# Mixing two expert branches as (x + a) + g (e − a), with −a added in PSUM and the ternary weight made at a later place

## The chip, the cores and the metric

The kernel runs on one core of a Trainium2 chip. The core has a matrix engine (PE), a vector engine (DVE), an activation engine (ACT), a general engine (POOL) and an engine that mainly issues transfers (SP). The metric is the device time of one launch in microseconds (us). All numbers here are us unless they say otherwise. A row such as `128x1024 f32` means 128 partitions with 1024 elements each.

## The reference, cut to what matters

Two layers on an input of 2 sequences of 2048 rows, 256 wide, all in float32. In the first layer attention and a mixture of experts work side by side on the normalised input; in the second a Mamba state space and a linear layer with a ternary weight do.

```python
xn = layernorm(x)
# first layer, feed-forward half (xn is normalised once more inside, with ln_g, ln_b)
abel   = gelu(xn2 @ abel_w + abel_b)                 # "a" in this text
moe    = sum over the two chosen experts of weight * expert(xn2)
nonabel = moe @ rot                                  # "e"; rot is a product of three matrix exponentials
g      = sigmoid(concat([abel, nonabel]) @ mix_w + mix_b)
ffn    = xn + abel * (1 - g) + nonabel * g
x      = x + attention(xn) + ffn

# second layer
xn = layernorm(x)
delta  = 0.7 * mean(abs(weight))
w_tern = where(weight > delta, 1, where(weight < -delta, -1, 0)) * alpha
x      = x + mamba(xn) + (xn @ w_tern.T + bias)
# mamba: projection to 1024, causal convolution over 4 rows, silu, projections for dt, B and C,
# a scan h = exp(dt A) h + dt B x over the rows for 512 channels and 16 states, y = sum h C + x D, gate, projection
```

## The kernel before, in words

Rows are tiled as 32 tiles of 128 rows, grouped in eight chunks of 512 rows (`QT` = 4 tiles). Four stages follow each other.

**The first stage** (0 to 183 in the profiled execution; the lines 180 to 319) loops over the eight chunks c. Each chunk is normalised twice (`n1`, `n2`; `normalised` at L144 issues four DVE tensor_scalar operations), transposed, and projected to q, k and v, which leave for DRAM or stay in SBUF. Its branch a is made by matmuls (L300, L307) and a GELU on ACT (L308) into `ab`. Then POOL multiplies `ab` by the gate's weights into `am` (L311), DVE sums `am` over its columns into `sab` (L314), SP spills `ab` to the DRAM array `ab_d` (L315), and POOL adds `n1` and the attention bias to the kept input `xa` (L316, L317). The buffers `ab` and `am` belong to a pool that ends with the stage; the next stage's constants lie in the same area.

**Attention** (183 to 1229) makes masks first (L595 to L635, on POOL) and then runs units written out by hand: the maxima of one unit (L665, L675, L678) are issued 22 units ahead of the exponentials and the values of another. SP reads q and k from DRAM for it (L554). It adds its result to `xa`.

**The experts** (1229 to 1876) take 37 tiles of gathered rows through two matrices of one expert each and write the results to `y_d`. `xa` goes out to `xa_d` there.

**Mixing and state space** (1876 to 3025; L1167 to L1893) works on eight units, one per chunk of 512 rows, the two sequences in turn. Three generators do the work of a unit: `mix(at)` gathers the experts' rows, scales and adds them, computes the gate and the mixed rows, and normalises and transposes them; `ahead(at)` projects, convolves and makes dt, B and C; `behind(at)` gates, projects and writes the output. The scan itself is a loop over 128 steps (8 units of 16 steps). In each step DVE runs a scan of 128x2048 (L1862) and the product that feeds a later one (L1772), POOL multiplies by C (L1874), PE sums over the states (L1789), and `steps(at, n, q)` advances the generators of the units that are one, two and three ahead at places in a table.

The order of the work has two regimes. Up to the line `ctx.enter_context(tc.manual_schedule())` (L1803) a planner orders each engine's instructions by program order and its own costs. Behind that line every engine, and every queue of transfers, runs in program order. What is issued there first is: all of `mixes[0]`; ten alternating pieces of `aheads[0]` and `mixes[1]` (its eight gathers and the scaling); the piece of `aheads[0]` that makes dt for the first 128 channels (L1513 to L1522); the 16 loads of C's rows by SP (`c_rows`, L1720); three more pieces of `mixes[1]` (POOL's sum L1335, the loads of `ab` and `xc` L1337 and L1339, and the transposes L1346); and a piece of `aheads[0]` that fills four blocks of a spreading matrix (DVE, L1526) and spreads dt by matmuls (L1536). Then comes the first step of the scan.

Inside `mix`, the gate's logits go through ACT (L1367, L1368) and a DVE reciprocal (L1374) to g, ACT forms 1 − g (L1375), PE multiplies the experts' rows by `rot` in two halves `pn` (L1381; one float32 matmul is two instructions in the trace), DVE adds g times each tile of `pn` to `xc` (L1388), ACT scales `ab` by 1 − g (L1395, four operations), and POOL adds it to `xc` (L1398). DVE's statistics (L1404) follow.

The ternary weight is made once, by the lines 1261 to 1275 in the setup ahead of the planner's end: a load of 256 KB on SP, an absolute value on ACT (L1264), a sum on DVE (L1266), a matmul with ones (L1268), and six DVE operations (L1270 to L1275). Its buffer `wt` shares a single place (tag `k`) with `ab` of each unit and with each unit's `n3`. Its first reader is the output projection of the first unit (L1621).

Of the kernel before, what the change touches and what calls it, by code (L numbers as in the profile page):

```python
# [11 lines left out]
F32 = mybir.dt.float32  # L12
F32R = mybir.dt.float32r
AF = mybir.ActivationFunctionType
ALU = mybir.AluOpType
AX = mybir.AxisListType
# [3 lines left out]
P = 128  # L20
B = 2
S = 2048
D = 256
# [78 lines left out]
def tile_model(ctx: ExitStack, tc: tile.TileContext, t, out):  # L102
    nc = tc.nc
# [15 lines left out]
    ident = const.tile([P, P], F32, name="ident")  # L119
    make_identity(nc, ident)  # L120
    ones = const.tile([P, P], F32, name="ones")
    nc.gpsimd.memset(ones, 1.0)
    rot = const.tile([P, 2, D], F32, name="rot")
# [27 lines left out]
    QT = CH // P  # L151
# [6 lines left out]
    with ExitStack() as c0:  # L158
# [5 lines left out]
        ab_d = scr.tile([P, NT, D], F32, name="ab_d")  # L164
# [3 lines left out]
        with tc.tile_pool(name="vs", bufs=1) as vsp, tc.tile_pool(name="qk", bufs=3) as qk:  # L168
# [6 lines left out]
            with tc.tile_pool(name="pa", bufs=2) as pa, tc.tile_pool(  # L175
                name="pa_w", bufs=1
            ) as pa_w, tc.tile_pool(name="pa_ps", bufs=3, space=PSUM) as pa_ps, tc.tile_pool(
                name="pa_pa", bufs=5, space=PSUM
            ) as pa_pa:
                for c in range(NCH):  # L180
                    xg = xa[:, c * QT : (c + 1) * QT, :]
# [13 lines left out]
                for name in ("q", "k"):  # L195
                    ws = pa_w.tile([P, 2, NG, P], F32, tag="ws", name=f"w{name}")
                    nc.sync.dma_start(ws, t[f"w{name}"])
                    wt = pa_w.tile([P, 2, D], F32, name=f"w{name}d")
# [20 lines left out]
                for c in range(NCH):  # L219
                    xg = xa[:, c * QT : (c + 1) * QT, :]  # L220
# [13 lines left out]
                    for k in range(2):  # L234
                        p1 = pa_ps.tile([P, CH], F32, tag="tr", name=f"p1_{c}_{k}")
                        p2 = pa_ps.tile([P, CH], F32, tag="tr", name=f"p2_{c}_{k}")
                        for i in range(QT):
# [8 lines left out]
                            scale=col("ln_g")[:, k : k + 1],  # L246
                            bias=col("ln_b")[:, k : k + 1],
# [4 lines left out]
                    for i, name in enumerate(("q", "k")):  # L252
                        for m in range(2):
                            ps = pa_pa.tile([P, CH], F32, tag="ab", name=f"{name}_{c}_{m}")
                            for k in range(2):
                                nc.tensor.matmul(
                                    ps,
                                    lhsT=wd[i][:, k, m * P : (m + 1) * P],
                                    rhs=x1[:, k, :],
                                    start=(k == 0),  # L260
                                    stop=(k == 1),
                                )
                            parts = pa.tile([P, 2, CH], F32R, tag="parts", bufs=3, name=f"{name}p_{c}_{m}")
                            bias = bd[i][:, m : m + 1]
# [11 lines left out]
                    for h in range(2):  # L276
                        ps = pa_pa.tile([P, 2, D], F32, tag="ab", name=f"v_{c}_{h}")
                        for j in range(2):
                            at = (2 * h + j) * P
                            for k in range(2):  # L280
                                nc.tensor.matmul(
                                    ps[:, j, :],
                                    lhsT=x1[:, k, at : at + P],
                                    rhs=wv[:, k, :],
                                    start=(k == 0),
                                    stop=(k == 1),
# [9 lines left out]
                    ab = pa.tile([P, QT, D], F32, tag="ab", name=f"ab_{c}")  # L296
                    for i in range(QT):
                        ps = pa_pa.tile([P, D + E], F32, tag="ab", name=f"abp_{c}_{i}")
                        for k in range(2):
                            nc.tensor.matmul(  # L300
                                ps,
                                lhsT=x2[:, k, i * P : (i + 1) * P],
                                rhs=aw[:, k, :],
                                start=(k == 0),
                                stop=False,
# [4 lines left out]
                    am = pa.tile([P, QT, D], F32, tag="am", name=f"am_{c}")  # L310
# [1 line left out]
                        am, ab, row("mix_w")[:, 0:D].unsqueeze(1).to_broadcast([P, QT, D]), ALU.mult  # L312
                    )
                    nc.vector.tensor_reduce(sab[:, c * QT : (c + 1) * QT], am, AX.X, ALU.add)  # L314
                    nc.sync.dma_start(ab_d[:, c * QT : (c + 1) * QT, :], ab)  # L315
                    nc.gpsimd.tensor_tensor(xg, xg, n1, ALU.add)  # L316
                    nc.gpsimd.tensor_tensor(  # L317
                        xg, xg, row("b_proj").unsqueeze(1).to_broadcast([P, QT, D]), ALU.add
                    )
# [847 lines left out]
def mix_and_state_space(tc, t, col, row, ident, ones, rot, routes, sab, rw, y_d, ab_d, xa_d, out_tiles):  # L1167
# [10 lines left out]
    nc = tc.nc  # L1178
    NC = S // CH
    QT = CH // P  # L1180
# [5 lines left out]
    with ExitStack() as ctx:  # L1186
        w = ctx.enter_context(tc.tile_pool(name="ss_w", bufs=1))
        one = ctx.enter_context(tc.tile_pool(name="ss_1", bufs=1))
# [7 lines left out]
        ps_m = ctx.enter_context(tc.tile_pool(name="ss_pm", bufs=2, space=PSUM))  # L1196
# [60 lines left out]
        eps = w.tile([P, 1], F32, name="eps")  # L1257
        nc.gpsimd.memset(eps, EPS)


        wt = one.tile([P, 2, D], F32, tag="k", name="wt")
        nc.sync.dma_start(wt, t["weight"])
        tern = w.tile([P, 2, D], F32, name="tern")
        nc.scalar.activation(tern, wt, AF.Abs)  # L1264
        part = w.tile([P, 1], F32, name="part")
        nc.vector.tensor_reduce(part, tern, AX.XY, ALU.add)  # L1266
        ps = ps_m.tile([P, 1], F32, tag="mm", name="absum")
        nc.tensor.matmul(ps, lhsT=ones, rhs=part, start=True, stop=True)  # L1268
        lim = w.tile([P, 2], F32, name="lim")
        nc.vector.tensor_scalar(lim[:, 0:1], ps, 1.0 / (D * D), 0.7, ALU.mult, ALU.mult)  # L1270
        nc.vector.tensor_scalar(lim[:, 1:2], lim[:, 0:1], -1.0, None, ALU.mult)
        nc.vector.tensor_scalar(tern, wt, lim[:, 0:1], None, ALU.is_gt)
        nc.vector.tensor_scalar(wt, wt, lim[:, 1:2], None, ALU.is_lt)
        nc.vector.tensor_tensor(tern, tern, wt, ALU.subtract)
        nc.vector.tensor_scalar(tern, tern, row("alpha"), None, ALU.mult)  # L1275

        carry, tail = [], []
        for b in range(B):
            cr = w.tile([P, NU, 4], F32, name=f"carry{b}")
# [13 lines left out]
        def mm(name, shape=(P, CH)):  # L1293
            settle(1)
            return ps_m.tile(list(shape), F32, tag="mm", name=name)
# [17 lines left out]
        def mix(at):  # L1313
# [36 lines left out]
                yield  # L1350
            settle()

            ps = mm(f"gate_{u}", (P, QT))
            nc.tensor.matmul(ps, lhsT=ident, rhs=sab[:, n0 : n0 + QT], start=True, stop=False)
            for i in range(QT):
# [16 lines left out]
            settle()  # L1372
            yield
            nc.vector.reciprocal(g[:, 0, :], g[:, 1, :])  # L1374
            nc.scalar.activation(g[:, 1, :], g[:, 0, :], AF.Identity, scale=-1.0, bias=1.0)  # L1375
            for h in range(2):
                ps = mm(f"pn_{u}_{h}", (P, 2, D))
                for i in range(2):
                    ts = slice((2 * h + i) * P, (2 * h + i + 1) * P)
                    for k in range(2):  # L1380
                        nc.tensor.matmul(  # L1381
                            ps[:, i, :], lhsT=moT[:, k, ts], rhs=rot[:, k, :], start=(k == 0), stop=(k == 1)
                        )

                def add(ps, h=h):
                    for i in range(2):
                        n = 2 * h + i
                        nc.vector.scalar_tensor_tensor(  # L1388
                            xc[:, n, :], ps[:, i, :], g[:, 0, n : n + 1], xc[:, n, :], ALU.mult, ALU.add
                        )  # L1390

                issued(ps, add)
                yield
            for i in range(QT):
                nc.scalar.activation(ab[:, i, :], ab[:, i, :], AF.Copy, scale=g[:, 1, i : i + 1])  # L1395
            yield
            settle()
            nc.gpsimd.tensor_tensor(xc, xc, ab, ALU.add)  # L1398
            yield

            mv = one.tile([P, QT, 2], F32, tag="mv", bufs=2, name=f"mv3_{u}")
# [314 lines left out]
        def c_rows(at, g):  # L1716

            cc = bcp.tile([P, 1, CH], F32, tag="cc", name=f"cc_{at}_{g}")
            for r in range(4):
                nc.sync.dma_start(  # L1720
                    cc[C4 * r : C4 * (r + 1), 0, :], of[at]["c_d"][4 * g + r].partition_broadcast(C4)
                )
            of[at]["cc", g] = cc
# [74 lines left out]
        def taken(G):  # L1798
            if G >= 0 and G % 4 == 3:
                at, n = divmod(G, NU)  # L1800
                nc.scalar.copy(of[at]["xs"][:, n // 4, :], of[at]["y"])

        ctx.enter_context(tc.manual_schedule())  # L1803
        mixes = [mix(at) for at in range(len(units))]
        aheads = [ahead(at) for at in range(len(units))]
# [5 lines left out]
        next(aheads[0])  # L1811
        for g in range(4):
            c_rows(0, g)
        for _ in range(3):
            next(mixes[1])
        next(aheads[0])
# [169 lines left out]
```

## Time and profile before

| | |
|---|---|
| median of 3 runs | 3027.67 (3023.68 to 3031.63) |
| the profiled execution's own time | 3027.19 |
| its span | 3025.5 |
| its mean granted PE clock | 0.908 |
| PE, DVE, ACT, POOL busy in the span | 2616.7, 2063.7, 1592.7, 1159.4 |

By stage, busy time and granted clock:

| stage | span | PE | DVE | ACT | POOL | clock | DMA share |
|---|---|---|---|---|---|---|---|
| first stage | 0–183 | 143.4 | 107.4 | 73.3 | 60.9 | 0.94 | 0.82 |
| attention | 183–1229 | 989.9 | 864.6 | 649.7 | 137.9 | 0.98 | 0.25 |
| experts | 1229–1876 | 618.1 | 121.4 | 167.1 | 107.8 | 0.98 | 0.47 |
| start of the last stage | 1876–1953 | 38.8 | 22.5 | 33.0 | 23.5 | 0.68 | 0.34 |
| first scan steps | 1953–2100 | 107.8 | 102.8 | 93.5 | 90.6 | 0.77 | 0.26 |
| the rest of the scan | 2100–3025 | 718.7 | 845.0 | 576.1 | 738.8 | 0.81 | 0.44 |

A timeline row has start, duration, engine, line, operation, the tiles written and read, shape, and in brackets how long the engine had been idle and what released it. A row of the chain of waits has start, duration, engine, tile and line of one piece of the path that ended last. PEld is the loading of weights into PE, which runs beside its matmuls; SPq and ACTq are issues of transfers.

### The profile page before, as it was taken

What the parts mean: (1) busy time and instruction counts of PE and PEld (TensorE: products, weight loads), DVE (VectorE), ACT (ScalarE), POOL (GpSimd) and SP (SyncE); (2) the same over time, 40 slices, a digit from 0 to 9 for tenths busy, and PEclk for the clock granted to TensorE, in tenths of its full rate; (3) what the DMA queues carried; (4) which work ended last, traced back from release to release, by engine and by line L of the source; (5) the groups of instructions that cost most, each with busy time, mean ns of one, the idle gap of its engine ahead of it and who ended that gap; (6) DMA issues with size and microseconds to landing.
All of it is one profiled execution on the core that took longest, in us unless ns stands there. A gap on an engine that the chain in (4) does not pass through costs nothing. (4 is left out here: it accounts for less than half of the span.)

```text
span 3025.5 us, 39961 instructions
## 1 busy us (share of the span) xinstructions
PE 2616.7 (86%) x15021; PEld 1484.5 (49%) x15021; DVE 2063.7 (68%) x2630; ACT 1592.7 (53%) x2546; POOL 1159.4 (38%) x864
## 2 busy tenths in 40 slices
PE   6879999999999999799999997677878788887846
PEld 4544444445444444587888886332333243333313
DVE  6569888887888886232110101368999999999996
ACT  3425666665666666321322222466766666766542
POOL 4302221110001101111112111268897887978875
PEclk9969999999999999899999998787887878889758
DMA  8842432232222300543445554124443635445340
GB/s 294 209 145 68 85 76 50 41 45 50 36 29 37 49 2 15 183 139 125 149 165 183 193 187 110 59 68 95 116 109 87 153 76 126 105 98 132 81 108 14
DMA packets 120614, 309.58 MB, mean 102 GB/s; under 512 B 28464, under 2 KB 70832, under 8 KB 102880
## 3 DMA queue, kind: packets, MB, share of 16 engines
q1 hardware_dynamic: 100496, 206.57, 29.0%
q0 software_dynamic: 18576, 99.24, 9.7%
q8 instruction: 122, 2.00, 0.3%
q10 hardware_dynamic: 1344, 1.16, 0.1%
q14 instruction: 76, 0.62, 0.1%
HBM read 228.51 MB, written 78.38 MB: 101 GB/s over the span
## 5 line engine op out<-in xcount | busy, mean ns | idle before, releaser
L776 ACT ACTIVATE p<-s 128x1024 f32<-128x1024 f32 (+3 forms) x640 | 564.3, 900 | 337.9 <-PE s L763 256.3
L678 DVE TENSOR_REDUCE best<-m 128x2 f32<-128x1024 f32 (+3 forms) x640 | 670.7, 1063 | 68.4 <-PE m L665 58.6
L1874 POOL TENSOR_TENSOR hh<-hh,cc 128x2048 f32<-128x2048 f32 x128 | 580.0, 4531 | 10.4 <-POOL carry L1873 0.2
L1862 DVE TENSOR_TENSOR_SCAN hh<-decay,uh 128x2048 f32<-128x2048 f32 x128 | 565.9, 4421 | 22.7 <-ACT decay L1748 9.6
L718 PE MATMUL pv<-p,v 128*17 128x256 f32 (+1 forms) x4608 | 377.6, 373 | 4.3 <-ACT raw L749 3.8
L1748 ACT ACTIVATE decay<-dd,a_neg 128x511 f32<-128x511 f32 x512 | 332.9, 712 | 54.6 <-DVE hh L1862 54.0
L1137 ACT ACTIVATE hT<-h,b1s 128x256 f32<-128x256 f32 x296 | 137.6, 473 | 384.4 <-PE h L1130 384.3
L781 POOL TENSOR_SCALAR_AFFINE_SELECT p<-p 128x256 f32<-128x256 f32 x184 | 74.4, 406 | 664.6 <-ACT p L776 663.9
L1151 DVE TENSOR_TENSOR yt<-o,b 128x512 f32<-128x512 f32 x37 | 25.6, 692 | 437.4 <-PE o L1143 437.4
L1772 DVE TENSOR_TENSOR uh<-dd,bb 128x2048 f32<-128x2048 f32 x128 | 293.6, 2294 | 19.7 <-PE bb L1759 10.7
L665 PE MATMUL m<-k,q 64*128 64x512 f32 (+3 forms) x1280 | 281.5, 424 | 27.4 <-ACT p L776 15.2
L763 PE MATMUL s<-q,k 64*128 64x512 f32 (+3 forms) x1280 | 285.9, 433 | 21.7 <-DVE best L678 17.7
L1130 PE MATMUL h<-xT,w 128*128 128x256 f32 x1184 | 276.1, 387 | 19.5 <-ACT hT L1137 7.7
L1143 PE MATMUL o<-w,hT 128*128 128x256 f32 x1184 | 262.1, 379 | 0.0
L1093 POOL DMA_INDIRECT w<-in_w,wrow x74 | 71.2, 962 | 478.1 <-PE h L1130 255.0
L1130 PEld LDWEIGHTS h<-xT,w 128*128 128x128 f32 x1184 | 227.0, 194 | 54.7 <-issue 8.4
L763 PE MATMUL s<-tops,onesr 64*128 64x512 f32 (+3 forms) x1280 | 247.3, 367 | 0.0
L1143 PEld LDWEIGHTS o<-w,hT 128*128 128x128 f32 x1184 | 225.2, 190 | 30.7
L1789 PE MATMUL y<-hh,sel 128*32 128x512 f32 x1024 | 163.7, 716 | 76.8 <-POOL hh L1874 76.6
L763 PEld LDWEIGHTS s<-q,k 64*128 64x128 f32 x1280 | 125.0, 185 | 167.7 <-DVE best L678 58.5
L665 PEld LDWEIGHTS m<-k,q 64*128 64x128 f32 x1280 | 127.3, 188 | 146.5 <-ACT p L776 88.8
L718 PEld LDWEIGHTS pv<-p,v 128*17 128x17 f32 x4608 | 106.8, 96 | 181.5 <-issue 114.0
(344 smaller groups left out, 3492.6 us busy)
## 6 DMA issues: line engine op xcount, KB each, us to landing
dd<-dd_d SPq DMA_DIRECT2D x120, 512.0 KB
q<-qk_d SPq DMA_DIRECT2D x128, 128.0 KB
k<-qk_d SPq DMA_DIRECT2D x128, 128.0 KB
x_d<-zero SPq DMA_DIRECT2D x6, 1664.0 KB
xg<-x_d SPq DMA_DIRECT2D x37, 256.0 KB
y_d<-yt SPq DMA_DIRECT2D x37, 256.0 KB
qk_d<-qp SPq DMA_DIRECT2D x16, 512.0 KB
qk_d<-kp SPq DMA_DIRECT2D x16, 512.0 KB
```

Source lines behind the costliest of these rows:

```text
L665: nc.tensor.matmul(ps[:, h, 0:n], lhsT=qT[hs, qs], rhs=kT[hs, c * CH : c * CH + n], start=True, stop=True, tile_position=(HP * h, 0),)
L678: nc.vector.tensor_reduce(best[:, i, :, c], ps[:, :, 0:n], AX.X, ALU.max)
L718: nc.tensor.matmul(pv[r0 : r0 + HS + 1, lo - f * HC : HC], lhsT=v[:, b * TPB + kb, 2 * pr + h, :], rhs=pt[:, h, lo:hi], start=(kb == 0), s ...
L763: nc.tensor.matmul(ps[:, h, off:CH], lhsT=(kT[hs, kb * P : (kb + 1) * P], onesr[hs, :])[i], rhs=(qT[hs, j * CH + off : (j + 1) * CH], tp[h ...
L776: nc.scalar.activation(pt[:, :, off:CH], ps[:, :, off:CH], AF.Exp, scale=float(HS) ** -0.5)
L1130: nc.tensor.matmul(ph, lhsT=w1[:, k * DF + f * P : k * DF + (f + 1) * P], rhs=xT[:, k, :], start=(k == 0), stop=(k == 1),)
L1143: nc.tensor.matmul(po[:, h, :], lhsT=hT[:, f, h * P : (h + 1) * P], rhs=w2[:, f * D : (f + 1) * D], start=(f == 0), stop=(f == NF - 1),)
L1748: nc.scalar.activation(decay[G % 2][:, q, 1:], of[at]["dd", n // 4][:, 0, q, 1:], AF.Exp, scale=a_neg[:, q, n : n + 1],)
L1772: nc.vector.tensor_tensor(uh, of[at]["dd", n // 4][:, 1], of[at]["bb", n].to_broadcast(full), ALU.mult)
L1789: nc.tensor.matmul(of[at]["y"][C4 * q : C4 * (q + 1), :], lhsT=sel, rhs=hh[:, q, :], start=False, stop=(g == 3), tile_position=(0, C4 * q),)
L1862: nc.vector.tensor_tensor_scan(hh.rearrange("p q c -> p (q c)"), decay[G % 2].rearrange("p q c -> p (q c)"), uh.rearrange("p q c -> p (q c)"),
L1874: nc.gpsimd.tensor_tensor(hh, hh, m_["cc", g].to_broadcast(full), ALU.mult)
```

## The change

Per unit the result is now formed as (x + a) + g (e − a). Three edits go together.

In the first stage ACT negates `ab` into `am` after `am` has been summed, SP spills `am` instead of `ab` (so `ab_d` holds −a), and POOL adds `ab` to the kept input, so `xa` holds x + a from there on. In the mix the operation 1 − g, the four scalings and POOL's addition are gone; in their place four matmuls with the identity add −a to `pn` in PSUM, one ahead of each tile's pair of matmuls with `rot`. The block that makes the ternary weight is put into a function that is called behind the manual schedule's start, between the 16 loads of C's rows and the three pieces of `mixes[1]`.

```diff
@@ first stage, per chunk
                     nc.vector.tensor_reduce(sab[:, c * QT : (c + 1) * QT], am, AX.X, ALU.add)
-                    nc.sync.dma_start(ab_d[:, c * QT : (c + 1) * QT, :], ab)
+                    nc.scalar.activation(am, ab, AF.Copy, scale=-1.0)
+                    nc.sync.dma_start(ab_d[:, c * QT : (c + 1) * QT, :], am)
                     nc.gpsimd.tensor_tensor(xg, xg, n1, ALU.add)
+                    nc.gpsimd.tensor_tensor(xg, xg, ab, ALU.add)
@@ mix, per unit
             nc.vector.reciprocal(g[:, 0, :], g[:, 1, :])
-            nc.scalar.activation(g[:, 1, :], g[:, 0, :], AF.Identity, scale=-1.0, bias=1.0)
             for h in range(2):
                 ps = mm(f"pn_{u}_{h}", (P, 2, D))
                 for i in range(2):
                     ts = slice((2 * h + i) * P, (2 * h + i + 1) * P)
+                    nc.tensor.matmul(
+                        ps[:, i, :], lhsT=ident, rhs=ab[:, 2 * h + i, :], start=True, stop=False
+                    )
                     for k in range(2):
                         nc.tensor.matmul(
-                            ps[:, i, :], lhsT=moT[:, k, ts], rhs=rot[:, k, :], start=(k == 0), stop=(k == 1)
+                            ps[:, i, :], lhsT=moT[:, k, ts], rhs=rot[:, k, :], start=False, stop=(k == 1)
                         )
...
-            for i in range(QT):
-                nc.scalar.activation(ab[:, i, :], ab[:, i, :], AF.Copy, scale=g[:, 1, i : i + 1])
             yield
             settle()
-            nc.gpsimd.tensor_tensor(xc, xc, ab, ALU.add)
             yield
@@ the ternary weight, out of the setup and into a function
-        wt = one.tile([P, 2, D], F32, tag="k", name="wt")
-        nc.sync.dma_start(wt, t["weight"])
...
+        def ternary():
+
+            wt = one.tile([P, 2, D], F32, tag="k", name="wt")
+            nc.sync.dma_start(wt, t["weight"])
+            tern = w.tile([P, 2, D], F32, name="tern")
+            nc.scalar.activation(tern, wt, AF.Abs)
+            part = w.tile([P, 1], F32, name="part")
+            nc.vector.tensor_reduce(part, tern, AX.XY, ALU.add)
+            ps = ps_m.tile([P, 1], F32, tag="mm", name="absum")
+            nc.tensor.matmul(ps, lhsT=ones, rhs=part, start=True, stop=True)
+            lim = w.tile([P, 2], F32, name="lim")
+            nc.vector.tensor_scalar(lim[:, 0:1], ps, 1.0 / (D * D), 0.7, ALU.mult, ALU.mult)
+            nc.vector.tensor_scalar(lim[:, 1:2], lim[:, 0:1], -1.0, None, ALU.mult)
+            nc.vector.tensor_scalar(tern, wt, lim[:, 0:1], None, ALU.is_gt)
+            nc.vector.tensor_scalar(wt, wt, lim[:, 1:2], None, ALU.is_lt)
+            nc.vector.tensor_tensor(tern, tern, wt, ALU.subtract)
+            nc.vector.tensor_scalar(tern, tern, row("alpha"), None, ALU.mult)
+            return tern
@@ the calls behind the manual schedule's start
         for g in range(4):
             c_rows(0, g)
+        tern = ternary()
         for _ in range(3):
             next(mixes[1])
         next(aheads[0])
```

More of the change, by code (lines that the diff above doesn't have):

```diff
@@ L1258, in mix_and_state_space @@
         nc.gpsimd.memset(eps, EPS)
-        wt = one.tile([P, 2, D], F32, tag="k", name="wt")
-        nc.sync.dma_start(wt, t["weight"])
[L1263 to L1275, printed above, removed]
         carry, tail = [], []
```

## The prediction

> **What bounds the kernel now.** I read the page's busy shares and slices first, then stretches by stage, then the chain of waits and each engine's instructions around every edit.
>
> ```profile
> PE 2616.7 (86%) x15021; PEld 1484.5 (49%) x15021; DVE 2063.7 (68%) x2630; ACT 1592.7 (53%) x2546; POOL 1159.4 (38%) x864
> DVE  6569888887888886232110101368999999999996
> POOL 4302221110001101111112111268897887978875
> ```
>
> PE's 86% is an average of stages with different limits; DVE and POOL are full only in the last third. The stretches (us; busy PE, PEld, DVE, ACT, POOL; then granted clock) show attention, a first-stage part and one scan chunk:
>
> ```profile
> 183.00:1229.00 1046.00, 989.93 (x8807) 474.88 (x8807) 864.58 (x1477) 649.72 (x978) 137.87 (x255) 0.98 0.25 45
> 90.00:110.00 20.00, 19.87 (x87) 14.35 (x85) 16.42 (x51) 10.38 (x18) 7.09 (x3) 1.00 0.88 179
> 2358.00:2487.00 129.00, 106.37 (x349) 46.46 (x347) 121.07 (x67) 87.38 (x138) 108.67 (x58) 0.84 0.47 111
> ```
>
> The first stage is PE's (19.87 of 20), attention PE's, the scan DVE's (121 of 129) with POOL close behind (109). The change touches the first stage, the start of the last stage, and each scan chunk. The sum is made against the profiled run's own time, 3027.19 (span 3025.5 and 1.7 around it), 0.5 below the median of the three runs, 3027.67.
>
> **First stage: a negation and one more POOL add per chunk (8 chunks).** What matters most is the end of the stage, in the timeline:
>
> ```profile
> 178.50 0.34 SPq L315 DMA_DIRECT2D ab_d<-ab  x1
> 178.55 2.35 POOL L311 TENSOR_TENSOR am<-ab,rows 128x1024 f32<-128x1024 f32 x1 [12.01 <-ACT ab L308]
> 180.93 1.22 DVE L314 TENSOR_REDUCE sab<-am 128x4 f32<-128x1024 f32 x1 [2.26 <-POOL am L311]
> 182.26 0.29 POOL L595 MEMSET mask<- 128x128 f32 x1 [1.36 <-DVE sab L314]
> 182.98 0.76 DVE L675 TENSOR_TENSOR m<-m,mask 128x256 f32<-128x256 f32 x2
> ```
>
> The attention mask is written into space that the stage has given back, so it waits for the stage's last reader: here the reduction, ending 182.15. Now the spill of ab leaves from am, behind product, reduction and negation. The negation is one ACT operation of 128x1024: 1.05, between the 0.63 that ACT takes for 128x512 and 1.48 for 128x1536. So: reduction 182.15, negation 183.25, spill issued 183.3; the old spill, issued 178.50, had landed by 182 (at most 3.6; I take 3.3), so am is free at 186.6 and the mask starts 4.4 later. Nothing hides that: mask, first masked scores and first maxima hang on it, and DVE is busy 20.00 of 20 in 190–210, so it isn't made up. **+4.4**. POOL's two adds (2.35 each, 180.9 to 185.6) end before it. Lower end 0, if the allocator puts the mask elsewhere; the upper end is a rival.
>
> Inside the stage the new POOL add (2.35) makes POOL's work 9.5 in a chunk of 16.5, so POOL itself has room; DVE pays when both meet:
>
> ```profile
> 63.48 2.37 POOL L311 TENSOR_TENSOR am<-ab,rows 128x1024 f32<-128x1024 f32 x1 [6.76 <-ACT ab L308]
> 64.22 1.78 DVE L144 TENSOR_SCALAR n<-xa,mv_a,ra 128x256 f32<-128x256 f32 x1 [0.62 <-PE p L239]
> 67.05 1.05 DVE L144 TENSOR_SCALAR n<-xa,mv_a,ra 128x256 f32<-128x256 f32 x3
> ```
>
> Three of DVE's normalisations take 1.05 together; one that met the POOL operation took 1.78 alone and ended with it, so 1.4 was lost. The next chunk's normalisation now has one more such operation beside it. DVE is 1.3–2 ahead of PE in a chunk, which covers most: I take four chunks by 0.5, **+2** (0 if the slack covers all, +8 if four chunks lose 2.0).
>
> The Trainium skill, page "SBUF — State Buffer", section "Who interferes with whom", says that DVE's fast two-port forms and GpSimd share one port pair, held whole by whoever starts first. The 1.78 agrees, and the rule speaks against moving an add to POOL here. By it a chunk could lose the whole 2.35, eight chunks 18.8, where the row's 1.4 gives 11.2; the sum above uses neither, since PE sets the pace.
>
> **The ternary block moved.** In the setup it stood in front of the first mix:
>
> ```profile
> 1892.77 0.61 ACT L1264 ACTIVATE tern<-wt 128x512 f32<-128x512 f32 x1
> 1894.31 0.56 PE L1268 MATMUL absum<-part,ones 128*128 128x1 f32 x2 [21.15 <-DVE part L1266]
> 1894.72 1.95 PE L1346 MATMUL moT<-ident,ys 128*128 128x128 f32 x8
> 1896.92 0.49 DVE L1275 TENSOR_SCALAR tern<-tern,rows 128x512 f32<-128x512 f32 x1
> ```
>
> Its matmul held the mixer's transposes until 1894.72, though POOL's sum, their input, was ready at 1893.34: 1.3 to gain. From the first operation to the last the block takes 4.64 (1892.77 to 1897.41). Its new place:
>
> ```profile
> 1944.24 7.49 SPq L1720 DMA_DIRECT2D cc<-c_d  x16
> 1951.70 0.63 DVE L1526 COPY spare<-ident 128x128 f32<-128x128 f32 x4
> 1951.85 0.34 SPq L1337 DMA_DIRECT2D ab<-ab_d  x1
> 1952.07 2.05 PE L1536 MATMUL over<-dt,spare 128*128 128x512 f32 x2 [6.96 <-DVE spare L1526]
> ```
>
> Behind the manual schedule each engine keeps program order. SP issues the weight's load only after its 16 row loads, in ab's place at 1951.85. In the setup that load was issued at 1889.74 and Abs ran at 1892.77, at most 3.0 later; 1.75 is the shortest wait of a load's first data here; I take 2.7. So Abs at 1954.5, end of the block at 1959.2. On DVE the copies of L1526 stand behind it, on PE their matmuls and unit 1's transposes, on ACT the transposes' copies. All wait, and the first scan waits for the spread matmuls: they start near 1959.5 for 1952.07. **+7.4** (6.7 to 7.8). Nothing in front covers it. SP's next loads (ab, xc of unit 1) slip to 1958.6 and land near 1962, before their first use after 1974: 0, and the same slip as the rest if that cover were gone.
>
> **The mix itself, unit 0.** The chain of waits runs through it:
>
> ```profile
> 1900.55 6.30 PE pn L1381 x16
> 1906.88 0.89 DVE xc L1388 x2
> 1907.80 0.09 issue
> 1907.89 2.35 POOL xc L1398
> 1910.26 0.44 DVE st L1404
> ```
>
> Eight identity matmul instructions more: +2.7 to +3.8 at the 0.33–0.47 that one took here. The POOL add goes: −2.4. ACT's five scalings aren't in the chain: 0. With the 1.3 from the transposes: −1.3 + 3.2 − 2.4 = −0.5; half of the added eight belong to pn of the second half, which runs while DVE adds the first, so 0.8 less: **−1.3** (−2.5 to −0.3).
>
> **Units 1 and 2** run in the first chunk. Unit 1's statistics waited 5.78 for POOL's add, but the next DVE operation waits for ACT's unchanged chain: 0. Unit 2's waited 1.81 for it, and the longer pn gives 0.7 back: **−1.1** (−1.9 to +0.5).
>
> **Units 3 to 7**, one per scan chunk:
>
> ```profile
> 2314.56 3.78 PE L1381 MATMUL pn<-rot,ys 128*128 128x256 f32 x8
> 2318.38 0.88 DVE L1388 SCALAR_TENSOR_TENSOR xc<-pn,g,xc 128x256 f32<-128x256 f32 x2 [0.63 <-PE pn L1381]
> 2330.65 2.37 POOL L1398 TENSOR_TENSOR xc<-xc,ab 128x1024 f32<-128x1024 f32 x1
> ```
>
> DVE already waits for PE's pn, with the scan behind it in its queue. Four more instructions before that point cost 0.95 (0.24 each, as the second half's eight in 1.99) to 1.87 (0.47, as here): 1.4. POOL's add of 2.37 goes, but POOL's next product needs a scan ending 2333.7 and its carry copy is then held by a DVE operation, so 1.0 of the 2.37 comes through. 1.4 − 1.0 = +0.4, five times: **+2** (−4 to +9.4).
>
> Sum: 4.4 + 2 + 7.4 − 1.3 − 1.1 + 2 = +13.4, so 3027.2 + 13.4 = 3040.6; I say 3040.
>
> **Rivals.**
> POOL is the bound in the scan (ends not slower): POOL's add is in the chain of waits in seven units, POOL is 109 of 129 busy, and its product feeds PE's y sums. Then 2.35 comes off whole seven times, −16.5 for the +0.9 of units 1 to 7: 3027.2 + 12.5 − 16.5 = 3023. From 1.8 per unit on it ends below before. Against it: DVE is busier (121), and POOL has 4.7 of work in a step of 7.2.
> The spill queues on SP behind attention's reads: up to 14 q and k reads stand at 178.89–197.13, 0.46 to 1.8 each. If the planner leaves them ahead of the late spill, the mask waits up to 18 for 4.4: 3054. For it: the old spill went out 0.4 before the first of them. Against: the planner knows the spill's readiness only from its own costs, and program order favours the spill.
> PE becomes the bound in the scan: the added matmuls at 0.47 each, nothing back from POOL, 5 x 1.87 = +9.4 for +2: 3048. For it: clock 0.84 there and PE 106 of 129; against: 23 idle.
> The ternary block is hidden: would need the weight ahead of the row loads; SP's order, fixed, excludes that, so I give it nothing.
>
> **How the numbers follow.** About 0.3% (9) is what a measurement of this kernel can tell from no change: slower from 3036.8, faster below 3018.6. My forecast 0.50 (own range 3033 to 3047, 0.14 of it within 0.3%), POOL rival 0.20 (0.06 of it faster, 0.14 within), SP rival 0.15, PE rival 0.15. Faster 0.07 with a stray 0.01, same 0.28, slower 0.65. The range: 3026 leaves out half of the POOL rival, 3055 the tail of the SP rival, under 0.2 together.
>
> **What would show it.** The mask's memset near 186.6 instead of 182.3, with SP's spill before it; normalisations of 1–2.5 beside POOL in the first stage; Abs some 2.7 after SP's weight issue, behind the row loads, and the spread matmuls 7.4 later against the first cv; no POOL add in the mix, statistics that don't wait for POOL; DVE's xc waiting 1.6 to 2.5 for pn. Wrong would be: DVE idle in the scan shrinking by 2 per chunk (POOL rival), or the planner reordering the first stage, where PE stands idle 9.85 at 143.8–153.6 for SP and transfers, an order that any edit can tip either way.

## The result and the profile after

The changed kernel takes 3043.51 (median of 6, 3040.63 to 3047.33) against 3028.09 (median of 6) for the kernel before: a ratio of 1.0052, 95% interval 1.0040 to 1.0064, so 15.4 slower. The forecast was 3040 in a range of 3026 to 3055. The profiled execution of the changed kernel took 3043.13, with a span of 3041.4 (3025.5 before), so the two traces differ by 15.9.

Because nearly every engine waits for another at some place, the cleanest comparison is a ledger: the start of the same instruction in both traces (one profiled execution of each kernel), and how its lateness grows from one to the next.

| event | before | after | late by | grown by |
|---|---|---|---|---|
| POOL's product of the last chunk | 178.55 | 182.45 | 3.90 | +3.90 |
| mask's memset | 182.26 | 190.63 | 8.37 | +4.47 |
| last maximum of attention (DVE) | 1194.85 | 1203.52 | 8.67 | +0.30 |
| second group of weight gathers (experts) | 1240.30 | 1251.29 | 10.99 | +2.32 |
| last output of an expert (DVE) | 1873.19 | 1883.71 | 10.52 | −0.47 |
| POOL's sum of the first unit | 1891.00 | 1902.06 | 11.06 | +0.54 |
| its transposes | 1894.72 | 1904.45 | 9.73 | −1.33 |
| its statistics | 1910.26 | 1917.79 | 7.53 | −2.20 |
| projection ahead of dt (xp) | 1936.45 | 1943.72 | 7.27 | −0.26 |
| spread matmuls | 1952.07 | 1966.70 | 14.63 | +7.36 |
| first scan | 1965.66 | 1979.90 | 14.24 | −0.39 |
| scan of step 16 | 2131.60 | 2145.22 | 13.62 | −0.62 |
| last scan (step 127) | 2993.07 | 3007.72 | 14.65 | +1.03 |
| end of the span | 3025.5 | 3041.4 | 15.9 | +1.25 |

The end of the first stage, in the timeline after (start, duration, engine, line, operation):

```profile
182.45 2.35 POOL L311 TENSOR_TENSOR am<-ab,rows 128x1024 f32<-128x1024 f32 x1 [7.25 <-ACT ab L308]
184.76 2.35 POOL L318 TENSOR_TENSOR xa<-xa,ab 128x1024 f32<-128x1024 f32 x1
184.84 1.22 DVE L314 TENSOR_REDUCE sab<-am 128x4 f32<-128x1024 f32 x1 [2.26 <-POOL am L311]
186.09 1.06 ACT L315 ACTIVATE am<-ab 128x1024 f32<-128x1024 f32 x1 [3.71 <-DVE sab L314]
187.17 0.34 SPq L316 DMA_DIRECT2D ab_d<-am  x1
...
190.63 0.20 POOL L597 MEMSET mask<- 128x128 f32 x1 [1.10 <-DMA ab_d<-am]
```

The negation follows the reduction (1.06 for the 1.05 of the forecast), the spill follows the negation, and the mask is released by that spill, as its bracket says: 190.63 − 182.45 = 8.18 behind the product, where it was 3.71. SP issues the spill as soon as the negation ends; the read for attention that SP had issued before it, at 179.74, didn't hold it, so the forecast's rival in which the spill queues behind those reads did not come about.

The ternary block at its new place, and the first unit's mix, in the timeline after:

```profile
1917.00 0.88 DVE L1376 SCALAR_TENSOR_TENSOR xc<-pn,g,xc 128x256 f32<-128x256 f32 x2 [1.72 <-PE pn L1369]
1917.79 0.42 DVE L1389 BATCH_NORM_STATS2 st<-xc 128x6 f32<-128x256 f32 x1
...
1959.18 0.36 SPq L1791 DMA_DIRECT2D wt<-in_weight  x1
1961.82 0.63 ACT L1793 ACTIVATE tern<-wt 128x512 f32<-128x512 f32 x1 [4.25 <-DMA wt<-in_weight]
...
1965.93 0.49 DVE L1804 TENSOR_SCALAR tern<-tern,rows 128x512 f32<-128x512 f32 x1
...
1966.70 2.04 PE L1521 MATMUL over<-dt,spare 128*128 128x512 f32 x2 [1.02 <-DVE spare L1511]
```

The statistics start as soon as DVE has added the weighted sum; no POOL operation stands between. SP issues the weight at 1959.18, the absolute value comes 2.64 later, and the spread matmuls are released by DVE's copies behind the block.

### The profile page after: what moved, and what is told of

Same layout as the page of the kernel before. It is cut to its first block, busy times and chain, and to the rows that moved or that the text cites. A ratio compares the mean times of both kernels' runs of the same rounds, so it can differ in the third digit from the quotient of the medians.

```text
span 3041.4 us, 40044 instructions
## 1 busy us (share of the span) xinstructions
PE 2624.0 (86%) x15085; PEld 1496.1 (49%) x15085; DVE 2070.9 (68%) x2630; ACT 1588.5 (52%) x2514; POOL 1163.0 (38%) x864
## 3 DMA queue, kind: packets, MB, share of 16 engines
q10 hardware_dynamic: 1344, 1.16, 0.1%
## 5 line engine op out<-in xcount | busy, mean ns | idle before, releaser
L1879 POOL TENSOR_TENSOR hh<-hh,cc 128x2048 f32<-128x2048 f32 x128 | 580.1, 4532 | 10.3
L1132 PE MATMUL h<-xT,w 128*128 128x256 f32 x1184 | 277.2, 388 | 17.8 <-PEq L478 7.1
```

What stands on the lines that cost most here:

```text
L1132: nc.tensor.matmul(ph, lhsT=w1[:, k * DF + f * P : k * DF + (f + 1) * P], rhs=xT[:, k, :], start=(k == 0), stop=(k == 1),)
L1879: nc.gpsimd.tensor_tensor(hh, hh, m_["cc", g].to_broadcast(full), ALU.mult)
```

## The experiments

All times are compared with the kernel before, run beside each; "late by" is from the ledgers of the profiled executions.

**The block back in the setup** (the rest of the change kept).

```diff
         nc.gpsimd.memset(eps, EPS)
+        wt = one.tile([P, 2, D], F32, tag="k", name="wt")
+        nc.sync.dma_start(wt, t["weight"])
...
         for g in range(4):
             c_rows(0, g)
-        tern = ternary()
```

> The changed kernel with the ternary block back in the setup, ahead of the planner's end; nothing else is undone. Theory (the block stands bare in front of the first scan, 7.4 from the last of the 16 row loads to its last operation): the spread matmuls start 7.4 sooner against the reduction that feeds them, and the transposes of the first unit wait for the block's matmul again, 1.3 later; time 3043.5 - 7.4 + 1.3 = 3037.4. Rival (the block's place is absorbed, because the scan that follows makes up a late start): 3043.5.

Measured: 3039.92 for 3027.86, ratio 1.0040 (1.0025 to 1.0055), so 12.1 above the kernel before, 3.3 less than the whole change. In the ledger the 7.36 at the spread matmuls is gone (−0.01) and the transposes wait for the block's matmul (+1.09 for −1.33): as expected. The time shows only half of the 6.1 that was expected. In its trace the first stage ended 2.6 later (a product at 185.03 for 182.45), although PE's order there is the same; and the intervals of the two kernels against the kernel before overlap, so these times alone don't tell 6.1 from 3.3. The trace speaks against the rival (absorbed), and the next run tests it by its time.

**The block alone**, in the kernel before (its lines in the setup go, as in the change).

```diff
         for g in range(4):
             c_rows(0, g)
+        tern = ternary()
```

> The kernel before with one part of the change alone: the ternary block at the change's place, behind the 16 row loads. Theory: +7.4 in front of the spread matmuls, and 1.3 to 2.6 off the first transposes, which no longer wait for the block's matmul: the span's events at the spread matmuls stand 5 to 6 later against the last expert output than before, time 5.4 above the kernel before. Rival (absorbed by the scan): no difference.

Measured: 3038.21 for 3026.24, ratio 1.0028 (1.0015 to 1.0040), which is 4.5 to 12.1 above. In the ledger +7.39 at the spread matmuls, −1.33 at the transposes; from the last expert output to the spread matmuls 6.1 later. The expected 5.4 lies in the interval and the rival's zero doesn't: the scan doesn't absorb the block. Its trace even loses 4.2 more from the first scan to the last, with the mix of the kernel before; why was not looked into.

**The first stage alone**, with the old mix (ACT scales −a by g) and the block in the setup.

```diff
             for i in range(QT):
-                nc.scalar.activation(ab[:, i, :], ab[:, i, :], AF.Copy, scale=g[:, 1, i : i + 1])
+                nc.scalar.activation(ab[:, i, :], ab[:, i, :], AF.Copy, scale=g[:, 0, i : i + 1])
```

> The first stage of the changed kernel (negation, spill of -a, POOL's added sum), the ternary block in the setup, and the old mix (ACT scales -a by g, POOL adds it, no identity matmuls). Theory (the first stage costs 8.4 by the time the mask is made, and attention and the scan neither make it up nor add to it): 3028.1 + 8.4 = 3036.5, and up to 2 more if PE is granted half its clock at the end of attention again, as it was in the changed kernel. Rival (the added cost is in the mix: PE becomes the bound in the scan, and the first stage is made up in attention): 3028 to 3030.

Measured: 3040.53, ratio 1.0039 (1.0025 to 1.0053), which is 7.6 to 16.0 above, its centre higher than the 8.4 that was expected, and all of it above the rival. The mask's memset is late by 11.68: the wait for the spill is the same (+4.45), the stage itself costs more (+7.23 at the last product, from a first product at 52.04 for 52.05).

**The new mix alone** (first stage of before).

```diff
-                nc.scalar.activation(g[:, 1, :], g[:, 0, :], AF.Identity, bias=1.0)
+                nc.scalar.activation(g[:, 1, :], g[:, 0, :], AF.Identity, scale=-1.0, bias=neg)
...
+        nc.vector.tensor_scalar(rot, rot, -1.0, None, ALU.mult)
```

> The first stage of before, the ternary block in the setup, and the new mix, with the sign moved from a to g and rot (rot is negated once in the setup, g comes out as -g), so that no negated copy of a is needed. It leaves out the addition of a to x, so the result lacks it. Theory (the mix gives 2.2 at the start and nothing in the scan, where DVE sets the pace): 3026, between 3024 and 3028. Rival POOL (its removed addition comes off whole in seven units, 16.5, and 2.2 at the start): 3009. Rival PE (four more matmul instructions before DVE's addition at 1.87 in five units): 3035.

Measured: 3028.07 for 3027.86, ratio 1.0003 (0.9991 to 1.0014). 2.03 are gained from the first matmul of pn to the first statistics and given back later (+0.79 over the scan, +1.26 at the output behind it). Both rivals fall, since the interval runs from 2.7 below to 4.2 above: the POOL sum that goes isn't worth 16, the matmuls that come don't cost 7.

**The spill from ab itself** (no negation; sum of x and a kept).

```diff
-                    nc.scalar.activation(am, ab, AF.Copy, scale=-1.0)
-                    nc.sync.dma_start(ab_d[:, c * QT : (c + 1) * QT, :], am)
+                    nc.sync.dma_start(ab_d[:, c * QT : (c + 1) * QT, :], ab)
```

> The changed kernel without the negation: SP spills a itself, right after the GELU as before, and the sign sits in g and rot (negated once). POOL's added sum stays, the ternary block stays at its new place. Theory A (the mask waits for the last of two things, the spill out of am and POOL's own queue): without the late spill POOL's two additions, which end at 189.5 in the changed kernel, are next, so the mask's memset comes at 189.6 for 190.6, and the time falls by 1.1 only, to 3042.4. Rival B (the late spill alone holds the mask): the mask comes right behind the reduction, 4.5 sooner, 3039.

Measured: 3043.26, ratio 1.0048 (1.0034 to 1.0062). From the product to the mask's memset 7.05, for 8.18 in the changed kernel: 1.13 sooner, as theory A says. Its timeline shows who is next:

```profile
187.45 2.38 POOL L318 TENSOR_TENSOR xa<-xa,rows 128x1024 f32<-128x1024 f32 x1
189.77 0.23 POOL L596 MEMSET mask<- 128x128 f32 x1
```

POOL's two sums stand in front of the memset on its own queue. Taking away the late spill alone is worth 1.1 in the trace, not 4.5; the time, 10.3 to 18.8 above the kernel before, can't tell the one from the other.

**Without POOL's added sum** (x lacks a).

```diff
                     nc.gpsimd.tensor_tensor(xg, xg, n1, ALU.add)
-                    nc.gpsimd.tensor_tensor(xg, xg, ab, ALU.add)
```

> The changed kernel without POOL's added sum of x and a in the first stage; negation, late spill, new mix and the ternary block's new place stay. It leaves out the addition of a to x. Theory (in the first stage DVE's normalisations stand still while POOL's two sums run back to back, 4.4 for four instead of 1.4): the normalisations take 1.4 again, the last chunk's product starts at 178.5 to 180.6 (182.5 to 185.8 in the programs with the sum), the wait of 4.5 for the late spill stays, time 3043.5 - 4 = 3039.5. Rival (the first stage is late because of the negation on ACT or another order of the work): product at 182.5 or later, 3043.5.

Measured: 3039.71 for 3025.28, ratio 1.0046 (1.0033 to 1.0059). The time, 10.0 to 17.8 above the kernel before, doesn't tell the theories apart; the stage does. Four normalisations take 1.38 again, and the eight chunks from the first product to the last take 127.58, for 134.06 in the changed kernel. But its first product came at 53.72 for 48.39, so the stage's end is only 1.15 sooner: 181.30, above the 178.5 to 180.6 that were expected and below the rival's 182.5. The negation is still there, so it isn't what slows the stage, and the mask still waits for the spill (+4.33 at the memset) with POOL's second sum gone. The end of attention and the end of the program cost 2.41 and 1.16 more than before here too.

**The bias sum moved to attention**, ahead of the output projection (with the block behind the convolution, below).

```diff
-                    nc.gpsimd.tensor_tensor(
-                        xg, xg, row("b_proj").unsqueeze(1).to_broadcast([P, QT, D]), ALU.add
-                    )
...
         def output(b, j, attn):
+            xg = xa[:, b * TPB + j * QT : b * TPB + (j + 1) * QT, :]
+            nc.gpsimd.tensor_tensor(xg, xg, bias.unsqueeze(1).to_broadcast([P, QT, D]), ALU.add)
```

> As the run before it (block behind the convolution), and POOL's sum with the attention bias goes from the first stage to attention, one per 512 rows ahead of the output projection, so that POOL has three operations per chunk in the first stage again. Theory (POOL's fourth operation is what the first stage pays for, and POOL is idle in attention): last product back to 178.5 to 180.6, mask 2.35 sooner behind it, nothing lost in attention: 3035.9 - 4 - 2.3 = 3029.6. Rival (the sums block DVE in attention as they did in the first stage, 2.35 each, eight times): 3029.6 + 18.8 = 3048.

Measured: 3034.41 for 3025.28, ratio 1.0032 (1.0020 to 1.0045). The expectation failed, 133.17 from the first product to the last, and one line of its timeline says why:

```profile
104.45 2.35 POOL L797 TENSOR_TENSOR xa<-xa,rows 128x1024 f32<-128x1024 f32 x1
```

L797 is written in attention, and it runs at 104: the planner took the sums back into the first stage, to the same place behind the other sum. The kernel didn't do what its text says.

**The bias sum behind DVE's addition of the attention output**, which it then depends on.

```diff
                 nc.vector.tensor_tensor(xa[:, n0 : n0 + 2, :], xa[:, n0 : n0 + 2, :], po, ALU.add)
+                nc.gpsimd.tensor_tensor(
+                    xa[:, n0 : n0 + 2, :], xa[:, n0 : n0 + 2, :],
+                    bias.unsqueeze(1).to_broadcast([P, 2, D]), ALU.add)
```

> As the kernel with the bias sums in attention, but behind DVE's addition of the attention output, so that the planner cannot take them back into the first stage as it did. Theory (what the first stage pays is how long POOL's sums stand in a row behind the product, where DVE's normalisations come): with one sum behind the product instead of two, four normalisations take about 2.5 (1.4 before, 4.4 in the changed kernel), the first stage from the first to the last product 129 (126.5 before, 133.2 to 134.1 with two sums in a row), the mask's memset 2.3 sooner; time 3036.6 - 4.5 - 2.3 = 3029.8, and up to 2 more at the end of attention. Rival (the number of POOL operations is what counts, or another order): 133 or more again.

Measured: 3024.48 for 3026.24, ratio 0.9993 (0.9985 to 1.0002): not to be told from the kernel before, and 12 below the same kernel with the sums in the first stage (3036.60, the next experiment). The stage takes 125.87 from the first product to the last, less than the 126.50 of before. The timeline of one chunk in the kernel before, in the changed kernel, and in this one:

```profile
99.83 1.37 DVE L144 TENSOR_SCALAR n<-xa,mv_a,ra 128x256 f32<-128x256 f32 x4
```

```profile
99.26 2.39 POOL L318 TENSOR_TENSOR xa<-xa,ab 128x1024 f32<-128x1024 f32 x1
...
100.50 4.39 DVE L144 TENSOR_SCALAR n<-xa,mv_a,ra 128x256 f32<-128x256 f32 x4
...
101.73 2.36 POOL L319 TENSOR_TENSOR xa<-xa,rows 128x1024 f32<-128x1024 f32 x1
```

```profile
98.25 2.36 POOL L317 TENSOR_TENSOR xa<-xa,ab 128x1024 f32<-128x1024 f32 x1
...
99.47 2.26 DVE L144 TENSOR_SCALAR n<-xa,mv_a,ra 128x256 f32<-128x256 f32 x4
...
101.81 2.35 POOL L316 TENSOR_TENSOR xa<-xa,n 128x1024 f32<-128x1024 f32 x1 [1.20 <-DVE n L144]
```

With two sums in a row DVE's first normalisation ends with the first sum and the second with the second (4.39 for four); with one, only the first is held (2.26); with none there, 1.37. This run takes one operation out of the stage besides parting the two, and no run has all four of a chunk apart from each other, so the rival by the number of operations isn't tested by it alone. But POOL has three operations a chunk here and in the kernel before, and the normalisations take 2.26 here and 1.37 there: what counts for them is which operation runs at the same time. The mask's memset is 2.3 nearer to the product than in the kernel that this one builds on (4.71 for 7.05). Two more parts were not expected: attention is 4.1 shorter than in the kernel before (see the last section), and the passage from it to the experts' outputs 3.3 shorter, whose cause was not looked into. So the 12 are more than the stage's 8.3 and the mask's 2.3, and the time alone doesn't measure the sums.

**The block behind the convolution's matmuls**, with a spilled as it is.

```diff
+        for i in range(2 * NB + 2):
             next(aheads[0])
+            if i == 2 * NB - 1:
+                tern = ternary()
             next(mixes[1])
```

> As the kernel that spills a itself (3043.3), with the ternary block called after the eighth of the ten alternating pieces, behind the convolution's matmuls and ahead of the silu, where SP is idle, DVE has nothing and PE waits 4.0 for ACT. Theory (the block costs only what stands bare at its place): the weight has landed long before, the block runs beside the silu's table load, the spread matmuls come 7.4 sooner, 3035.9. Rival (the block carries its cost with it: its matmul and ACT's absolute value push the chain convolution, silu, projection): 3039 or more.

Measured: 3036.60 for 3025.28, ratio 1.0036 (1.0023 to 1.0049). The step at the spread matmuls is 0.00, where the kernel that spills a itself has +7.36. The block's matmul runs in front of PE's wait for the silu:

```profile
1940.00 0.28 PE L1799 MATMUL absum<-part,ones 128*128 128x1 f32 x2
```

**The same place in the kernel before.**

> The kernel before with the ternary block behind the convolution's matmuls, where the other run with that place showed no cost. Theory: only the gain at the transposes is left, 1.3 to 2.6 below the kernel before, the spread matmuls as much sooner against the last expert output. Rival (the scan's first steps wait for something else by then): no difference.

Its diff is the one above, on the kernel before. Measured: 3028.29, ratio 1.0009 (0.9998 to 1.0019). The trace has the 1.33 at the transposes and a step of 0.00 at the spread matmuls, but the times show no gain: from 0.6 below to 5.7 above the kernel before. The sum was a miss; that the block costs nothing at this place rests on the two traces.

**POOL's sum of x and a inside the mix, beside the gate** (first stage of before, block behind the convolution).

```diff
             issued(ps, sigmoid)
             yield
             settle()
+            nc.gpsimd.tensor_tensor(xc, xc, ab, ALU.add)
             yield
```

> A kernel with the first stage of before, the ternary block behind the convolution, and the new mix in another order: POOL adds a to x in the mix itself, as soon as both have landed and beside the gate, instead of behind the weighted sum; PSUM gets the subtraction of a through the sign of g and rot. Theory (POOL's sum costs only where the statistics wait for it, and the first stage and the block cost nothing here): 2.1 off the first mix, 1.4 to 2.7 off the transposes, 3028 - 4 = 3024, between 3022 and 3027. Rival (POOL sets the pace, and an earlier sum pushes its products): 3028 or more.

Measured: 3031.05 for 3025.28, ratio 1.0013 (1.0003 to 1.0023): slower, a miss. From the first gather of the last stage to the first scan it is 0.5 sooner than before, and from the first scan to the last it loses 4.7, 2.83 in one step alone:

```profile
2193.86 0.88 DVE L1378 SCALAR_TENSOR_TENSOR xc<-pn,g,xc 128x256 f32<-128x256 f32 x2 [3.16 <-PE pn L1371]
```

DVE waits 3.16 for pn, not for POOL: the twelve instructions of that half of pn took 5.5 there, at a granted clock of 0.50. So in this step the rival on POOL isn't what the trace shows either. Nor can the 4.7 be put down to the sum's new place: the kernel with the block alone and the old mix lost 4.2 over the same steps, the one with the bias sums moved to attention 4.7.

**The new mix in the first unit alone** (old mix elsewhere; block behind the convolution).

```diff
+                    if at == 0:
+                        nc.tensor.matmul(
+                            ps[:, i, :], lhsT=ident, rhs=ab[:, 2 * h + i, :], start=True, stop=False
+                        )
...
+            if at:
+                nc.gpsimd.tensor_tensor(xc, xc, ab, ALU.add)
```

> The kernel before with the ternary block behind the convolution, and the new mix in the first unit alone, POOL's sum of x and a beside the gate; the other seven units mix as before (with the signs of g and rot turned). Theory (the mix gains only where nothing runs beside it, in the first unit): 1.3 to 2.6 off the transposes and up to 2.1 off the statistics, scan as before: 3 to 4 below the kernel before. Rival (the first unit's gain is lost in the scan, whose first chunk waits for other things): no difference.

Measured: 3031.27 for 3026.24, ratio 1.0009 (0.9998 to 1.0019). The trace has both gains (−1.33, −2.08), and the scan keeps them (late by −1.58 at its first step, −1.28 at its last), but the runs don't: no difference that can be told. None of these kernels is shown to beat the kernel before.

## Why the forecast was right, point by point

**The mask.** Forecast +4.4 by reduction, negation, spill and landing; measured +4.47, and +4.45, +4.45 and +4.33 in the three other kernels with the negation. The estimate of 1.05 for the negation was 1.06. The forecast had POOL's sums end 1.0 ahead of the spill, and 1.1 was measured. What it did not say is what follows from that: the price has two causes, and without the late spill 3.3 of it stays.

**The ternary block.** Forecast +7.4 (weight 2.7 after its issue, 4.64 for the block); measured +7.36 in the changed kernel and +7.39 alone. The absolute value started 2.64 after the weight's issue. The gain at the transposes, forecast 1.3, was 1.33.

**The first unit.** Here a term was mis-sized. The step held that the added matmuls would give back POOL's 2.4, −1.3 in all; measured −1.33 and −2.20, so −3.5. The 24 instructions of pn took 6.8 in the changed kernel, the 16 before 6.4: PE's granted clock was 1.00 over the last 3 us of them, where it was 0.65 before. In the changed kernel the seventh instruction is the last to take more than 0.38, before it was the thirteenth. Some of this is luck: in the nine other kernels that have the added matmuls in their first unit, the 24 took 6.9 to 8.3, and from the transposes to the statistics 0.5 to 2.1 were gained.

**The first stage.** Here the overlap was wrong: "four chunks by 0.5", +2, with DVE's lead over PE as cover and one more POOL operation beside the normalisations. It is not one. Before, POOL did a chunk's bias sum right behind its sum with `n1`, ahead of that chunk's product. Now the bias sum must follow the new sum, which needs a, so both stand in a row behind the product, and the normalisations of a later chunk meet both. They lose 3.0 in each of four chunks, not 0.5. The lead covers a part only: the steps from one product to the next grow by 1.0, 1.6, 1.8 and 1.8 in the first four (18.2 for 16.5 in the third) and by 1.5 in the other three together. From the first product to the last the six kernels with two sums in a row take 133.2 to 134.1, the seven without the added sum 126.2 to 127.6: +7, the price that the forecast had as its upper end of 8.

The ledger shows only +3.90, because the six start their first product about 2 sooner on the mean (48.4 to 52.3 for 51.7 to 53.7). The traces show where 1.4 of that comes from: with the bias sum gone from its old place, the second normalisation of the first chunk takes 1.36 in all six, where it took 2.73 to 2.75 in the seven, beside that sum. In the kernel before and in the changed one:

```profile
16.14 2.34 POOL L317 TENSOR_TENSOR xa<-xa,rows 128x1024 f32<-128x1024 f32 x1
16.86 2.73 DVE L144 TENSOR_SCALAR n<-n,mv_b,rb 128x256 f32<-128x256 f32 x4
```

```profile
16.86 1.36 DVE L144 TENSOR_SCALAR n<-n,mv_b,rb 128x256 f32<-128x256 f32 x4
```

The rest varies from kernel to kernel with PE's first projections to q and k, whose eight matmuls took 3.6 to 6.5. So at the stage's end the mean difference is 4.7 (184.45 for 179.80).

The Trainium skill, page "SBUF — State Buffer", section "Who interferes with whom", has this rule: the pair of ports is held for a whole instruction. The rows agree, 4.39, 2.26 and 1.37 with two, one and no sum beside them; the forecast cited the rule and then let the cover decide.

**The scan.** Forecast −1.1 in the first chunk and +0.4 in each later one. The first chunk has −1.91 in the step where the statistics had waited 1.81 for POOL, and gives part of it back elsewhere (−0.62 in all). In the later chunks the price is where it was forecast, at DVE's addition; one step of the kernel before, then the same one after:

```profile
2445.37 0.88 DVE L1388 SCALAR_TENSOR_TENSOR xc<-pn,g,xc 128x256 f32<-128x256 f32 x2 [0.36 <-PE pn L1381]
```

```profile
2460.27 0.88 DVE L1376 SCALAR_TENSOR_TENSOR xc<-pn,g,xc 128x256 f32<-128x256 f32 x2 [1.13 <-PE pn L1369]
```

The wait grows by 0.77 here, and by 0.96, 2.11, 0.55 and 1.50 in the four other chunks: 1.2 on the mean, within the forecast's 0.95 to 1.87. Six steps later 0.80 comes back, where DVE's wait for PE falls from 1.41 to 0.61, and 0.45 to 0.76 in three of the other four. That is the "1.4 less 1.0" of the forecast; over the later chunks the sum is +1.0 for the forecast's +2. Where PE was granted half its clock (0.50), the same wait was up to 3.2. The scan's total is no test of so small a term: from the first scan to the last the thirteen other kernels took 2.1 less to 4.7 more than the kernel before, those with the old mix 0.4 less to 4.2 more.

**What the forecast did not have.** 2.32 at the end of attention and 1.25 behind the last scan. Both are PE's matmuls at another granted clock. Behind the last scan the first eight matmuls with `w_out` took 3.5 for 2.2. The last group of the attention's output projection before and after:

```profile
1238.03 1.99 PE L811 MATMUL po<-wo,aT 128*128 128x256 f32 x8 [0.78 <-DVE xa L819]
```

```profile
1247.34 3.67 PE L813 MATMUL po<-wo,aT 128*128 128x256 f32 x8 [0.78 <-DVE xa L821]
```

The same eight instructions take 1.99 at a granted clock of 1.00 or 3.67 at 0.53. Three kernels had the long form (+2.3 to +2.4), the eleven others, before among them, the short one. All three negate a and spill it late, and of the kernels that do so only one had the short form. So a link with the change isn't excluded, though these instructions weren't changed. Two kernels whose attention came at the same time in the trace (the last maximum at 1202.4) had one form each. What decides was not found.

The near agreement of 13.4 with the measured 15.4 is thus partly luck. In the ledger, whose whole is 15.9, the first stage is 1.9 above its term, the first unit 2.2 below, the scan 0.5 below, the two stretches of PE's clock add 3.6 that no term had, and the rest takes 0.3.

## What to carry to other kernels

A run of DVE operations that meets POOL's pays for how many POOL operations stand in a row there (here 1.37, 2.26 and 4.39 for none, one and two), and POOL's share of busy time doesn't show it: POOL was idle for 7.9 just ahead of the chunk's product and the row behind it. Putting one of the two sums behind something that really held it back took the whole 7 of the stage away. Before one adds an operation, it's worth asking which others must now follow it: the new sum alone cost the stage nothing (125.87 with it, 126.50 before), the bias sum that had to stand behind it made the row. A sum written at a later place isn't later if a planner orders the instructions; here it took a dependency to move it. And a block whose operations are each short costs its whole length, load included, when it stands in program order in front of the only chain: here 7.4 at one place and nothing, by the traces, some 23 us earlier, where PE waits for ACT.

## What was not expected of the hardware

The same code of attention took 1012 to 1013 from the mask to the last maximum in eleven kernels and 1008 to 1009 in three (the two with the bias sums moved, and the one with the ternary block alone behind the convolution), and the first product of the first stage came between 48.4 and 53.7. The executions of one kernel spread by some 13 (the kernel before: 3021 to 3034 in 35 runs). Whether these differences and the two forms of the granted clock make up that spread isn't shown, since each kernel has one trace; but effects of 1 to 3 us could be read from rows alone.
